# The D term by channels, and a new place for the output product, in a two-layer chunked scan on one core

## The chip, the cores and the metric

The kernel runs on one core of one Trainium2 chip. The metric is the device time of one execution in microseconds (us). A core has five engines that run side by side, each with its own instruction queue: TensorE (PE, matrix products, with a part PEld that loads weights), VectorE (DVE), ScalarE (ACT), GpSimd (POOL) and SyncE (SP, which here only issues DMA transfers). Products land in PSUM, a small accumulator memory from which DVE and ACT read.

## The reference, cut to what matters

The whole program is a network of several stages on an input of 8 x 128 x 64 x 64 numbers (8 batches, 128 channels, 4096 tokens). The change lies in one of them, the second layer's convolution part, which is built from a selective scan called `_mamba`:

```python
def _mamba(x, in_w, in_b, conv_w, conv_b, A_log, D, dt_bias, rms_w, out_w, headdim, d_state):
    zxbcdt = x @ in_w.T + in_b
    z = zxbcdt[..., :di]
    xBC = zxbcdt[..., di:2 * di + 2 * d_state]
    dt = jax.nn.softplus(zxbcdt[..., -nh:] + dt_bias)
    xp = jnp.pad(xBC, ((0, 0), (K - 1, 0), (0, 0)))
    xBC = sum((xp[:, k:k + l, :] * conv_w[:, k] for k in range(K)))     # K = 3
    xBC = _silu(xBC + conv_b)
    xs = xBC[..., :di].reshape(b, l, nh, headdim)
    Bm, Cm = xBC[..., di:di + d_state], xBC[..., di + d_state:]
    A = -jnp.exp(A_log)
    y = _ssd(xs * dt[..., None], dt * A, Bm, Cm)
    y = y + D[None, None, :, None] * xs
    y = y.reshape(b, l, di) * _silu(z)
    y = y * jax.lax.rsqrt(jnp.mean(y * y, -1, keepdims=True) + 1e-05) * rms_w
    return y @ out_w.T

def _ssd(x, A, Bm, Cm, chunk):          # per chunk
    Acs = jnp.cumsum(A, axis=-1)
    Lmat = jnp.exp(_segsum(A))          # exp(Acs[l] - Acs[s]) for s <= l
    Yd = einsum(Cm, Bm, Lmat, x)        # inside a chunk
    states = einsum(Bm, exp(Acs[-1] - Acs), x)
    st = exp(Acs[-1]) * st + states     # chunk after chunk
    Yo = einsum(Cm, previous st, exp(Acs))
    return Yd + Yo
...
gf = _mamba(gf, sm_..., 8, 16) + gf     # once, 8 channels: the "seeds"
...
def cascade(xi):                        # 8 groups of 16 channels
    for i in range(2):
        xi = _mamba(xi, cm_...[i], 8, 64)
    return xi
ys = jax.vmap(cascade)(xs) + xs * skip_scale
```

The line that the change computes in another way is `y = y + D * xs`, the D term. `xs` is the part of the projection that went through the three-tap convolution and the silu; D is one number for each head.

## The kernel before, in words

*Stages.* The program runs, one after the other: the first layer (a scan step by step), routing and experts, a set-up of the second layer (`second_setup`, which calls `ssd_weights` L989 for two layers of the cascade, CM, and for the seeds, SM), the seeds (SM), the cascade (CM), and the second feed-forward part. The tiles of the two scans end in `_cm` and `_sm` in the profile. All the parts that the change touches are used by these two.

*Tiling of the cascade.* A batch has 16 segments of SC = 256 tokens, a segment has two chunks of 128. The 8 groups of channels are held side by side: two in one 128-partition tile for B, C and states (`g2` = 2, so NP = 4 such pairs), four in one for z and y (`gh` = 4, so NH = 2 halves). A pass of the loop in `cascade` (L1575 to L1598) treats one segment of layer 0 and, two segments behind it, one of layer 1: 128 segments, 130 passes.

*A segment.* `ssd_project` (L1079) makes a segment's inputs from `stk`, the three shifted copies of the input rows stacked over partitions, so that one product does projection and convolution together: B and C (`bc_p`, into `BC`), z (`z_p` L1106 to L1111, four products, one silu into `zs`, channels on partitions), then the token products (`tok_p` L1116 to L1128: x, B and the raw dt with tokens on partitions, into `tok` and `dtr`), then after the mark `"silu"` a table load, softplus to `dt`, and `dA` = dt x A. `ssd_exponents` (L1050) sums dA along the tokens with one product (`cs_p`), splits the sum into three bf16 parts on DVE (`csq`, `csr`, L1063 to L1066: a cast, a difference, a cast, a difference) and sends them out to HBM and back in as rows `ssA`, `ssB`. Back in `ssd_project`, small products give `dec_p` (weights `wd` of the states) and `cd_p`, and `eA_p`, six products that need `csq`, gives exp of the cumulative sum with channels on partitions.

*A chunk.* `ssd_chunk` (L1173): `g_p` (products of B and C, masked by DVE into `gm`), `pad` and `xw` (x times dt, x times the state weights, on DVE), `xD` (x times D, on GpSimd, L1203 to L1205). `decays` makes the differences of the cumulative sum with rows `ssA`, `ssB` (`ss_p`, bf16 products), and ACT's exp of them into E, two tiles for each half. `masked` (L1227) multiplies E by gm on DVE. `yo_s_p` holds two things in one bank: the products of the old state with C, and the new state sums; DVE adds the latter to the scaled old state and GpSimd copies it into block form (`Sd`, L1267). After the mark `"decays"` follow y (`inside`, L1229 to L1234): for each half the product of `xD` with the identity starts the accumulation in `y_p` and the products of E and `pad` continue it. DVE multiplies yo by `eA` (`yy`), adds y, multiplies by `zs`: `yz` (L1275 to L1287).

*The output of a segment.* `ssd_output` (L1289): square on ACT, mean by products (`ms_p`), reciprocal root, the product of yz with it on GpSimd (L1302), and the output product `o_p` (L1307, two products, one for each half). `output` in `cascade` (L1516) then copies o_p out: for layer 0 on ACT into `y1s` (L1528) and by DMA to HBM, from where the next layer's `stk` is loaded (`load(1, n)`, four DMAs in `tap_stack`); for layer 1 it loads the input rows (`ys`), and DVE does x times skip plus o_p into `ys`, sums it into `gms`, and a DMA stores it.

*What sets the order.* In the cascade only ACT's table loads are pinned against the silus and exps around them (`silus_done`); for the rest the code is written as generators, each `yield` giving the turn to another, and the loop of `cascade` says which generator goes on until which mark (`until`, `between`, `both`, `drain`; `slow` gives two turns for each one). A scheduler then orders each engine's queue by the order of writing and by when inputs are ready in its own model. `after(later, earlier)` (L303) adds a dependency that fixes only the order of issue. PSUM has eight banks: tag "a" has tiles of two banks, three buffers (`wide`), for bc, z, tok, g, ss, ms and eA; tag "b" has one bank, two buffers (`narrow`), for cs, dec, cd, yo_s, y and o, which take turns in the order of writing. A new tile of a tag waits until the last reader of the tile two turns (or three) back is done. HBM rows go through SP's one queue in its order of issue.

*A pass, as it runs.* Layer 0's chunk 0, layer 1's chunk 0, layer 0's chunk 1, layer 1's chunk 1. In the first half the next segment of layer 0 is projected, in the second the next one of layer 1. Layer 0's output comes in the second half, layer 1's (`late`) is spread over the first half of the next pass.

Of the kernel before, what the change touches and what calls it, by code (L numbers as in the profile page):

```python
# [9 lines left out]
F32 = mybir.dt.float32  # L10
# [121 lines left out]
def layout(inputs):  # L132
# [74 lines left out]
    for j in range(2):  # L207
        blk = np.zeros((128, 64), np.float32)
        for g in range(4):
            blk[g * 32 : g * 32 + 32, g * 16 : g * 16 + 16] = i[p1 + "cm_out_w"][j].T  # L210
        c.add(f"cm{j}_out", blk)
        c.add(f"cm{j}_rms", np.tile(i[p1 + "cm_rms_w"][j], 4))
        c.add(f"cm{j}_Alog", rows(i[p1 + "cm_A_log"][j]))
        c.add(f"cm{j}_D", rows(i[p1 + "cm_D"][j]))
    blk = np.zeros((4, SM.nh, SM.hd, 4, SM.co), np.float32)
    rms = np.zeros((4, SM.nh, SM.hd), np.float32)
    for g in range(4):
# [2 lines left out]
    c.add("sm0_out", blk.reshape(128, 4 * SM.co))  # L220
    c.add("sm0_rms", rms.reshape(128))
    c.add("sm0_Alog", rows(i[p1 + "sm_A_log"]))
    c.add("sm0_D", rows(i[p1 + "sm_D"]))

    sd = Pack(128)
    for n in ("seed_tok_b", "seed_detok_b"):
# [52 lines left out]
class Net:  # L279
# [5 lines left out]


    def mm(self, out, lhsT, rhs, start=True, stop=True):
        self.ordered(self.nc.tensor.matmul(out, lhsT=lhsT, rhs=rhs, start=start, stop=stop))  # L288

    def keep_warm(self, bank, n):  # L290

# [697 lines left out]
    def ssd_weights(self, pool, cfg, j):  # L989

        nc = self.nc
        n = f"{cfg.name}{j}"

        def part(i):
            o, m = self.at["stacked"][f"{n}_{i}"]
            return self.st[:, o : o + m]

        W = pool.tile([128, cfg.cols], F32, name=f"W_{n}")
        nc.vector.memset(W[96:], 0.0)
        self.tt(W[:KST], part(0), part(1), ALU.mult)  # L1000
        self.tt(W[:KST], W[:KST], part(2), ALU.add)
        negA = pool.tile([128, cfg.nh], F32, name=f"negA_{n}")
        self.act(negA, self.w(f"{n}_Alog"), AF.Exp)
        self.ts(negA, negA, -1.0, ALU.mult)
        D = pool.tile([128, cfg.g2, cfg.nh, cfg.hd], F32, name=f"D_{n}")
        for g in range(cfg.g2):
            nc.vector.tensor_copy(D[:, g], bc(self.w(f"{n}_D"), cfg.hd))
        wo = pool.tile([cfg.pz, cfg.gh * cfg.co], F32, name=f"wo_{n}")
        self.ts(wo, self.w(f"{n}_out")[: cfg.pz], self.w(f"{n}_rms")[: cfg.pz], ALU.mult)
        return {"W": W, "negA": negA, "D": D.rearrange("p g h q -> p (g h q)"), "wo": wo, "fill": 6 if cfg is SM else 0}  # L1010

    def ssd_rings(self, pool, cfg, n, npads, nrows, nstates):

# [36 lines left out]
    def ssd_exponents(self, cfg, dA, n_tok, ring, wk, ps, fill):  # L1050


        nc = self.nc
        NC, nh, G = n_tok // 128, cfg.nh, cfg.g
        n = NC * G * nh
        t_ = cfg.name
        p = ps.tile([128, S], F32, tag="b", bufs=self.narrow, name="cs_p")
        self.keep_warm(p, fill)
        p = p[:n, :128]
        self.mm(p, dA.rearrange("p c g -> p (c g)"), self.k("le"))  # L1060
        part = wk.tile([n, 3, 128], BF16, name=f"csq_{t_}")
        rest = wk.tile([n, 128], F32, name=f"csr_{t_}")
        nc.vector.tensor_copy(part[:, 0], p)  # L1063
        self.tt(rest, p, part[:, 0], ALU.subtract)
        nc.vector.tensor_copy(part[:, 1], rest)
        self.tt(part[:, 2], rest, part[:, 1], ALU.subtract)  # L1066
        d = self.dp.tile([3, n, 128], BF16, name=f"cs_{t_}", bufs=3)
        nc.sync.dma_start(d.rearrange("i n t -> n i t"), part)
        A, B = self.turn(ring, "row")
        g4 = cfg.g4  # L1070
        for r in range(g4):
            v = d.rearrange("i (c g h) t -> i c g h t", g=g4, h=nh)[:, :, r]
            nc.sync.dma_start(B[32 * r : 32 * r + 3], v)
            for i in range(3):
                o = 32 * r + 3 + i * nh
                nc.sync.dma_start(A[o : o + nh, :, r], v[i].rearrange("c h t -> h c t"))
        return A, B, part

    def ssd_project(self, cfg, W, ring, stk, n_tok, wk, ps):  # L1079
# [17 lines left out]
        for j0 in range(0, NP, per):  # L1097
# [5 lines left out]
            silus.append(self.act(BC[:, j0 : j0 + per].rearrange("p j x s -> p (j x s)"),  # L1103
                                  v.rearrange("p j x s -> p (j x s)"), AF.Silu))
            yield None
        zs = wk.tile([pz, NH, n_tok], F32, name=f"zs_{t_}", bufs=nl_)  # L1106
        p = ps.tile([128, 2, S], F32, tag="a", bufs=self.wide, name="z_p")
        for j in range(NP):
            o = (j * g2 % gh) * hi
            self.mm(p[o : o + g2 * hi, j * g2 // gh, :n_tok], Wp[:, cfg.o_z : cfg.o_z + g2 * hi], stk(j))  # L1110
        silus.append(self.act(zs, p[:pz, :NH, :n_tok], AF.Silu))  # L1111
        yield None
        tok = wk.tile([128, NC, NP, cfg.wsil], F32, name=f"tok_{t_}", bufs=nb_)
        dtr = wk.tile([128, NC, NP, g2 * nh], F32, name=f"dtr_{t_}")
# [1 line left out]
        for c in range(NC):  # L1116
            p = ps.tile([128, 2, S], F32, tag="a", bufs=self.wide, name="tok_p")
            for j in range(NP):
                o = (j % ppb) * cfg.wtok
                self.mm(p[:, j // ppb, o : o + cfg.wtok], stk(j)[:, c * 128 : (c + 1) * 128],  # L1120
                        Wp[:, cfg.o_t : cfg.o_t + cfg.wtok])
            for q in range(nbk):
                v = p[:, q, : ppb * cfg.wtok].rearrange("p (j f) -> p j f", j=ppb)
                jj = slice(q * ppb, (q + 1) * ppb)
                silus.append(self.act(tok[:, c, jj, :], v[:, :, : cfg.wsil], AF.Silu))
                nc.vector.tensor_copy(dtr[:, c, jj, :], v[:, :, cfg.wsil :])  # L1126
            if c < NC - 1:
                yield None  # L1128
# [39 lines left out]
                    self.mm(p[:pz, hf, c * 128 : (c + 1) * 128], self.spread[: NC * GH, o : o + m], part[:, i],  # L1168
                            start=i == 0, stop=i == 2)
        self.act(eA, p[:pz, :NH, :n_tok], AF.Exp)  # L1170
        yield {"BC": BC, "zs": zs, "tok": tok, "dt": dt, "w": w, "cd": cd, "eA": eA, "ssA": ssA, "ssB": ssB, "n": n_tok}

    def ssd_chunk(self, cfg, W, st, sg, c, wk, ps):  # L1173

# [25 lines left out]
        xw = wk.tile([128, NP, g2 * nh, hd], F32, name=f"xw_{t_}")  # L1200
        self.tt(xw, x4, bc(w[:, c].rearrange("p (j g) -> p j g", j=NP), hd), ALU.mult)
        xw = xw.rearrange("p j g q -> p (j g q)")
        xD = wk.tile([128, NP, g2 * hi], F32, name=f"xD_{t_}")  # L1203
        self.tt(xD, xt, bc(W["D"], NP, 1), ALU.mult, nc.gpsimd)
        xD = xD.rearrange("p j q -> p (j q)")  # L1205
        yield None
        Es = [[], []]

# [18 lines left out]
                self.stt(f, f, 1.0, bc(gm[:, g0 * 128 : (g0 + ng) * 128], nh, 1), ALU.min, ALU.mult)  # L1227

        def inside(hf):  # L1229
            self.mm(y[:pz, hf], xD[:, hf * pz : (hf + 1) * pz], self.k("ident"), start=True, stop=False)  # L1230
            for h in range(nh):
                for g in range(gh):
                    self.mm(y[g * hi : (g + 1) * hi, hf], pad[:, hf * gh + g, h * hi : (h + 1) * hi],
                            Es[hf][g // ng][:, h, g % ng, :], start=False, stop=h == nh - 1)  # L1234

        old = st["S"]
        decays(0)
# [32 lines left out]
        yield "decays"  # L1270
        y = ps.tile([128, NH, 128], F32, tag="b", bufs=self.narrow, name="y_p")
        inside(0)
        if old is not None:
            yy = wk.tile([pz, NH, 128], F32, name=f"yy_{t_}")
            self.tt(yy, yo[:pz], sg["eA"][:, :, cs], ALU.mult)  # L1275
        masked(1)
        yield None
        inside(1)
# [1 line left out]
        if c == 0:  # L1280
            sg["yz"] = wk.tile([pz, NH, sg["n"]], F32, name=f"yz_{t_}")
        out = sg["yz"][:, :, cs]
        if old is None:
            self.tt(out, y[:pz], sg["zs"][:, :, cs], ALU.mult)
        else:
            self.tt(yy, yy, y[:pz], ALU.add)
            self.tt(out, yy, sg["zs"][:, :, cs], ALU.mult)  # L1287

    def ssd_output(self, cfg, W, sg, n_tok, wk, ps):  # L1289

# [13 lines left out]
        o = ps.tile([128, S], F32, tag="b", bufs=self.narrow, name="o_p")  # L1304
        n = gh * cfg.co
        for hf in range(NH):
            self.mm(o[hf * n : (hf + 1) * n, :n_tok], W["wo"], yz[:, hf])  # L1307
        yield o[: NH * n, :n_tok]

    def tap_stack(self, src, lo, first, ring):  # L1310
# [166 lines left out]
    def cascade(self, ps):  # L1477
# [5 lines left out]
        with tc.tile_pool(name="cs", bufs=1) as pl, tc.tile_pool(name="csw", bufs=2) as wk:  # L1483
# [32 lines left out]
            def output(layer, n):  # L1516
# [7 lines left out]
                if layer == 0:  # L1524
                    if k == 0:
                        y1[b] = self.dp.tile([C, L], F32, name="y1", bufs=2)
                    y = wk.tile([C, SC], F32, name="y1s")
                    nc.scalar.copy(y, o)  # L1528
                    nc.sync.dma_start(y1[b][:, sg], y)
                    load(1, n)  # L1530
                else:
                    x = wk.tile([C, SC], F32, name="ys")
                    nc.sync.dma_start(x, self.xs[b][:, sg])
                    self.stt(x, x, self.w("skip"), o, ALU.mult, ALU.add)
                    nc.vector.tensor_reduce(self.gms[:, b, k : k + 1], x, AX.X, ALU.add)
                    nc.sync.dma_start(self.ys[b][:, sg], x)
# [24 lines left out]
            def drain(*gens):  # L1561
                for g in gens:
                    for _ in g:
                        pass

            def slow(gen):

                for v in gen:
# [2 lines left out]

            load(0, 0)
            drain(project(0, 0))
            late = p = iter(())
            for n in range(total + 2):  # L1575
                x = [chunk(0, n, 0), chunk(1, n - 2, 0), chunk(0, n, 1), chunk(1, n - 2, 1)]
                until(x[0], "decays", [p])
# [3 lines left out]
                until(p, "silu")  # L1581
                drain(rest)
                until(x[1], "decays", [late])
                p = slow(p)
                next(p, None)
                until(x[1], "end", [p])
                until(x[2], "decays", [p])
                drain(p, late)
                p = project(1, n - 1)
                rest = between(x[2], x[3])  # L1590
                until(p, "silu")
                drain(rest)
                first = slow(output(0, n))
                until(x[3], "decays", [first])
                p = slow(p)
                next(p, None)
                until(x[3], "end", [p, first])
                late = both(first, slow(output(1, n - 2)))  # L1598
            drain(late)

    def second_ffn(self):

# [274 lines left out]
```

## Time and profile before

| what | value |
|---|---|
| three runs | 18963.84, 18971.56, 18972.04 us; median 18971.56 |
| the profiled execution's own time | 18991.37 us |
| its span (first to last record) | 18989.2 us |
| mean granted TensorE clock | 0.955 of full |
| busy share of PE, DVE, ACT, POOL | 85%, 81%, 59%, 48% |
| the seeds, 9487 to 10297 us | PE busy 664 of 810 us, DVE 467 |
| the cascade, 10420 to 17369 us | PE busy 6523 of 6949 us, DVE 5150, ACT 4657, POOL 1428 |

The shares over the whole span mix stages with different limits, so only the last row bears on the loop: it covers 128 passes. The busiest groups there, over 12000 to 16000 us (73 passes), each with its number of instructions, its busy time and the mean of one:

| group | engine | count | busy us | mean ns |
|---|---|---|---|---|
| E = min(E, 1) x gm, 128x1024 (L344) | DVE | 1167 | 1399.4 | 1233 |
| E = exp(ss_p), 128x1024 | ACT | 1168 | 1143.0 | 1028 |
| y_p from E and pad | PE | 18684 | 747.4 | 276 |
| ss_p | PE | 2336 | 642.5 | 381 |
| bc_p | PE | 2336 | 558.2 | 387 |
| tok_p | PE | 2336 | 434.2 | 339 |
| Sd copy, 64x128 (L1267) | POOL | 584 | 326.0 | 558 |
| xD, 128x256 | POOL | 292 | 307.3 | 1052 |
| y_p from xD and the identity | PE | 1166 | 255.2 | 301 |
| yz x sq, 128x512 (L1302) | POOL | 146 | 198.0 | 1356 |
| z_p | PE | 1168 | 158.3 | 392 |
| o_p | PE | 584 | 97.3 | 401 |
| zs = silu(z_p), 128x512 | ACT | 146 | 87.2 | 597 |

An fp32 product shows as several records, so a count here is larger than the number of products in the code. Products overlap in the pipeline, so the mean of one is more than the distance from one start to the next. Idle time of an engine is told with what ended it, "<-" and the releaser: "PE o_p <- POOL yz_cm" is time in which PE stood ahead of an o_p product until GpSimd's yz was done.

### The profile page before, as it was taken

Reading aid. Unit: us, or ns where it says so; the run is one execution under the profiler, and the core shown is the slowest. Engines: PE = TensorE matmul, PEld = TensorE weight load, DVE = VectorE, ACT = ScalarE, POOL = GpSimd, SP = SyncE. Lnnn points to the kernel's source line nnn. Section 1 sums busy time; section 2 is a strip of 40 time slices with the busy share of each in tenths; the row PEclk is TensorE's granted clock in tenths of the full one; section 3 lists DMA queues with packets and bytes.
Section 4 is the critical chain, followed back from the end, with each engine's and each line's share of the span. In section 5 each row is a group of like instructions: output and inputs, shape, how many; then the busy total and the mean of one; then the engine's idle time right before and its main releaser. Section 6 shows DMA issues by size and latency. Waiting matters only on the chain. (4 is left out here: it accounts for less than half of the span.)

```text
span 18989.2 us, 300098 instructions
## 1 busy us (share of the span) xinstructions
PE 16050.9 (85%) x114341; PEld 8381.8 (44%) x114341; DVE 15333.3 (81%) x20453; ACT 11238.5 (59%) x15902; POOL 9062.3 (48%) x6308
## 2 busy tenths in 40 slices
PE   6777777777777777777787999999999999998898
PEld 2222222222222222223644666666666666665343
DVE  6999999999999999998264777777777777776886
ACT  5555656565555656554254666666666666666553
POOL 6777777777777777774011122222222222222444
PEclk8999999999999999999697999999999999999999
DMA  3555554545555455554442011011111011011222
GB/s 108 141 142 141 141 141 137 144 139 137 143 138 138 135 145 136 137 136 119 136 145 66 27 30 30 28 30 30 28 30 29 28 30 29 28 30 37 91 94 82
DMA packets 843741, 1734.85 MB, mean 91 GB/s; under 512 B 184315, under 2 KB 416667, under 8 KB 833883
## 3 DMA queue, kind: packets, MB, share of 16 engines
q1 hardware_dynamic: 842302, 1715.66, 31.8%
q8 instruction: 904, 14.81, 0.3%
q14 instruction: 535, 4.38, 0.1%
HBM read 1474.28 MB, written 241.04 MB: 90 GB/s over the span
## 5 line engine op out<-in xcount | busy, mean ns | idle before, releaser
L335 POOL TENSOR_TENSOR bx<-xE,B 128x1024 f32<-128x1024 f32 x2048 | 4818.5, 2356 | 1032.3 <-DMA xE<-dtx_d 659.1
L288 PE MATMUL dA<-parts,expand 128*128 128x512 bf16 x12288 | 3192.5, 398 | 1846.3 <-DVE last L347 1383.8
L296 ACT ACTIVATE dA<-dA,negA 128x1024 f32<-128x1024 f32 x2048 | 2228.4, 1088 | 3224.5 <-PE dA L288 3118.6
L757 DVE TENSOR_TENSOR_SCAN dA<-dA,last,bx 128x1024 f32<-128x1024 f32 x1536 | 3609.3, 2350 | 108.5 <-POOL bx L335 90.3
L288 PEld LDWEIGHTS <-expand 128*128 128x128 bf16 x12288 | 1109.1, 100 | 4414.2 <-DVE last L347 2179.2
L296 ACT ACTIVATE E_cm<-ss_p 128x1024 f32<-128x1024 f32 x2048 | 2003.3, 1028 | 1301.1 <-PE ss_p L288 1301.0
L335 DVE TENSOR_TENSOR hc<-dA,C 128x1024 f32<-128x1024 f32 x2048 | 2507.7, 1224 | 70.4
L344 DVE SCALAR_TENSOR_TENSOR E_cm<-E_cm,gm_cm 128x1024 f32<-128x1024 f32 x2048 | 2454.7, 1233 | 86.0 <-ACT E_cm L296 45.4
L335 POOL TENSOR_TENSOR xD_cm<-tok_cm,D_cm 128x256 f32<-128x256 f32 x512 | 536.6, 1048 | 2759.8 <-PE y_p L288 2680.5
L1267 POOL COPY Sd_cm<-S_cm 64x128 f32<-64x128 f32 x1024 | 573.8, 560 | 2574.1 <-DVE S_cm L335 2467.1
L288 PE MATMUL y_p<-E_cm,pad_cm 128*32 128x128 f32 x32768 | 1316.6, 277 | 125.9 <-DVE E_cm L344 123.8
L288 PE MATMUL ss_p<-ssB_cm,ssA_cm 128*128 128x512 bf16 x4096 | 1132.1, 383 | 158.3 <-DVE gm_cm L335 96.6
L757 DVE TENSOR_TENSOR_SCAN dA<-dA,bx 128x1024 f32<-128x1024 f32 x512 | 1172.2, 2290 | 55.9 <-POOL bx L335 54.9
L288 PE MATMUL y<-hc,kt 128*32 128x512 f32 x8192 | 1207.6, 663 | 3.6 <-DVE hc L335 3.6
L1126 DVE COPY dtr_cm<-tok_p 128x16 f32<-128x16 f32 x1024 | 178.5, 174 | 1158.3 <-ACT tok_cm L296 1158.3
L288 PEld LDWEIGHTS y_p<-E_cm,pad_cm 128*32 128x32 f32 x32768 | 901.9, 109 | 429.8 <-DVE E_cm L344 247.5
L288 PE MATMUL bc_p<-stk_cm,W_cm 128*128 128x256 f32 x4096 | 985.4, 389 | 25.2 <-DMA stk_cm<-xs 20.8
L288 PEld LDWEIGHTS bc_p<-stk_cm,W_cm 128*128 128x128 f32 x4096 | 754.5, 191 | 196.4 <-issue 75.0
L288 PE MATMUL tok_p<-W_cm,stk_cm 128*128 128x200 f32 x4096 | 761.4, 339 | 0.0
L288 PE MATMUL g_p<-BC_cm 64*128 64x128 f32 x8192 | 753.1, 294 | 2.2 <-ACT E_cm L296 2.2
L296 ACT ACTIVATE tok_cm<-tok_p 128x384 f32<-128x384 f32 x1024 | 502.0, 490 | 398.2 <-PE tok_p L288 248.7
L288 PEld LDWEIGHTS tok_p<-W_cm,stk_cm 128*128 128x128 f32 x4096 | 682.5, 190 | 98.5 <-issue 98.1
(412 smaller groups left out, 29633.0 us busy)
## 6 DMA issues: line engine op xcount, KB each, us to landing
xE<-dtx_d SPq DMA_DIRECT2D x2048, 512.0 KB
dtx_d<-dtx SPq DMA_DIRECT2D x256, 256.0 KB
x<-x SPq DMA_DIRECT2D x256, 256.0 KB
pb<-p_d SPq DMA_DIRECT2D x64, 1024.0 KB
ssA_cm<-cs_cm SPq DMA_DIRECT2D x3072, 4.0 KB
stk_cm<-xs SPq DMA_DIRECT2D x368, 128.0 KB
stk_cm<-y SPq DMA_DIRECT2D x368, 128.0 KB
px<-in_x_dram SPq DMA_DIRECT2D x64, 256.0 KB
```

What stands on the lines that cost most here:

```text
L288: self.ordered(self.nc.tensor.matmul(out, lhsT=lhsT, rhs=rhs, start=start, stop=stop))
L296: i = self.ordered(self.nc.scalar.activation(out, in_, func, **kw))
L335: self.ordered((eng or self.nc.vector).tensor_tensor(out, a, b, op))
L344: self.ordered(self.nc.vector.scalar_tensor_tensor(out=out, in0=a, scalar=s, in1=b, op0=op0, op1=op1))
L757: self.ordered(nc.vector.tensor_tensor_scan(out=t, data0=t, data1=bx.pop(n), initial=0.0 if ch["j"] == 0 else last[:, q : q + 1], op0=ALU. ...
L1126: nc.vector.tensor_copy(dtr[:, c, jj, :], v[:, :, cfg.wsil :])
L1267: nc.gpsimd.tensor_copy(Sd[gr, :, g * hi : (g + 1) * hi], S2[gr])
```

## The change

The D term is computed with channels on partitions. D is packed with one number for each of the 128 partitions, and the tile D of before with its copies is dropped. `z_p` becomes twice as wide: after z's four products four more with the columns of x (`cfg.o_t`) fill its other half, and one silu over both gives `zx`, of which `zs` and `xT` (x with channels on partitions) are the halves. GpSimd multiplies xT by D once for each segment. In `ssd_chunk`, `xD` and the identity products go; the first y product of each head-0 group starts the accumulation; GpSimd adds xT to `yy` after DVE's yo x eA, and where there is no old state DVE adds xT to y itself, one operation more than before.

Two dependencies of issue order are added, both for the cascade alone: the first y product of a chunk stands behind the latest cumulative sum (`self.summed`), and the first output product behind the latest token product (`self.projected`). The loop lets layer 1's output go on for two steps only (`head`), drains the rest of it after the next token products of layer 1, and takes two steps of a projection right after the `"decays"` marks instead of one. `y1s` and `ys` share one ring of three buffers.

```diff
         c.add(f"cm{j}_Alog", rows(i[p1 + "cm_A_log"][j]))
-        c.add(f"cm{j}_D", rows(i[p1 + "cm_D"][j]))
+        c.add(f"cm{j}_D", np.tile(np.repeat(i[p1 + "cm_D"][j], CM.hd), CM.gh))
...
-        D = pool.tile([128, cfg.g2, cfg.nh, cfg.hd], F32, name=f"D_{n}")
-        for g in range(cfg.g2):
-            nc.vector.tensor_copy(D[:, g], bc(self.w(f"{n}_D"), cfg.hd))
...
-        self.mm(p, dA.rearrange("p c g -> p (c g)"), self.k("le"))
+        self.summed = self.mm(p, dA.rearrange("p c g -> p (c g)"), self.k("le"))
...
-        zs = wk.tile([pz, NH, n_tok], F32, name=f"zs_{t_}", bufs=nl_)
+        zx = wk.tile([pz, NH, 2, n_tok], F32, name=f"zx_{t_}", bufs=nl_)
         p = ps.tile([128, 2, S], F32, tag="a", bufs=self.wide, name="z_p")
-        for j in range(NP):
-            o = (j * g2 % gh) * hi
-            self.mm(p[o : o + g2 * hi, j * g2 // gh, :n_tok], Wp[:, cfg.o_z : cfg.o_z + g2 * hi], stk(j))
-        silus.append(self.act(zs, p[:pz, :NH, :n_tok], AF.Silu))
+        for x, w in enumerate((cfg.o_z, cfg.o_t)):
+            for j in range(NP):
+                o = (j * g2 % gh) * hi
+                self.mm(p[o : o + g2 * hi, j * g2 // gh, x * n_tok : (x + 1) * n_tok], Wp[:, w : w + g2 * hi], stk(j))
+        silus.append(self.act(zx.rearrange("p f x s -> p f (x s)"), p[:pz, :NH, : 2 * n_tok], AF.Silu))
+        zs, xT = zx[:, :, 0], zx[:, :, 1]
+        self.tt(xT, xT, bc(W["D"].to_broadcast([pz, n_tok]), NH, 1), ALU.mult, nc.gpsimd)
...
-                self.mm(p[:, j // ppb, o : o + cfg.wtok], stk(j)[:, c * 128 : (c + 1) * 128],
+                self.projected = self.mm(p[:, j // ppb, o : o + cfg.wtok], stk(j)[:, c * 128 : (c + 1) * 128],
                         Wp[:, cfg.o_t : cfg.o_t + cfg.wtok])
...
-        xD = wk.tile([128, NP, g2 * hi], F32, name=f"xD_{t_}")
-        self.tt(xD, xt, bc(W["D"], NP, 1), ALU.mult, nc.gpsimd)
-        xD = xD.rearrange("p j q -> p (j q)")
...
         def inside(hf):
-            self.mm(y[:pz, hf], xD[:, hf * pz : (hf + 1) * pz], self.k("ident"), start=True, stop=False)
             for h in range(nh):
                 for g in range(gh):
-                    self.mm(y[g * hi : (g + 1) * hi, hf], pad[:, hf * gh + g, h * hi : (h + 1) * hi],
-                            Es[hf][g // ng][:, h, g % ng, :], start=False, stop=h == nh - 1)
+                    i = self.mm(y[g * hi : (g + 1) * hi, hf], pad[:, hf * gh + g, h * hi : (h + 1) * hi],
+                            Es[hf][g // ng][:, h, g % ng, :], start=h == 0, stop=h == nh - 1)
+                    if cfg is CM and hf == h == g == 0:
+                        self.after(i, self.summed)
...
         inside(0)
+        yy = wk.tile([pz, NH, 128], F32, name=f"yy_{t_}")
+        xT = sg["xT"][:, :, cs]
         if old is not None:
-            yy = wk.tile([pz, NH, 128], F32, name=f"yy_{t_}")
             self.tt(yy, yo[:pz], sg["eA"][:, :, cs], ALU.mult)
+            self.tt(yy, yy, xT, ALU.add, nc.gpsimd)
...
-        if old is None:
-            self.tt(out, y[:pz], sg["zs"][:, :, cs], ALU.mult)
-        else:
-            self.tt(yy, yy, y[:pz], ALU.add)
-            self.tt(out, yy, sg["zs"][:, :, cs], ALU.mult)
+        self.tt(yy, yy if old is not None else xT, y[:pz], ALU.add)
+        self.tt(out, yy, sg["zs"][:, :, cs], ALU.mult)
...
-            self.mm(o[hf * n : (hf + 1) * n, :n_tok], W["wo"], yz[:, hf])
+            i = self.mm(o[hf * n : (hf + 1) * n, :n_tok], W["wo"], yz[:, hf])
+            if cfg is CM and hf == 0:
+                self.after(i, self.projected)
...
-                    y = wk.tile([C, SC], F32, name="y1s")
+                    y = wk.tile([C, SC], F32, name="ys", bufs=3)
...
-                    x = wk.tile([C, SC], F32, name="ys")
+                    x = wk.tile([C, SC], F32, name="ys", bufs=3)
...
+            def head(gen, k):
+                for _ in range(k):
+                    next(gen, None)
+                    yield None
+                    yield None
...
-            late = p = iter(())
+            late = out1 = p = iter(())
             for n in range(total + 2):
                 x = [chunk(0, n, 0), chunk(1, n - 2, 0), chunk(0, n, 1), chunk(1, n - 2, 1)]
                 until(x[0], "decays", [p])
...
                 until(x[1], "decays", [late])
+                next(p, None)
+                next(p, None)
                 p = slow(p)
-                next(p, None)
                 until(x[1], "end", [p])
                 until(x[2], "decays", [p])
                 drain(p, late)
                 p = project(1, n - 1)
                 rest = between(x[2], x[3])
                 until(p, "silu")
+                drain(out1)
                 drain(rest)
                 first = slow(output(0, n))
                 until(x[3], "decays", [first])
+                next(p, None)
+                next(p, None)
                 p = slow(p)
-                next(p, None)
                 until(x[3], "end", [p, first])
-                late = both(first, slow(output(1, n - 2)))
-            drain(late)
+                out1 = output(1, n - 2)
+                late = both(first, head(out1, 2))
+            drain(late, out1)
```

## The prediction

> **What bounds the kernel now.** I read the page first: span, busy slices, granted clock.
>
> ```profile
> span 18989.2 us, 300098 instructions
> ...
> PE   6777777777777777777787999999999999998898
> ...
> DVE  6999999999999999998264777777777777776886
> ...
> PEclk8999999999999999999697999999999999999999
> ```
>
> The change touches slices 20 to 36 alone: the seeds (9487 to 10297 us by the rows of E_sm) and the cascade. In the cascade PE stands at 9 in full clock. The 128 copies of L1528 start from 10419.8 to 17369.2 us: 6949.4/127 = 54.72 us per loop pass, and the passes are alike to 0.01 us away from batch edges. One pass therefore stands for the stage. Next the stretch table (us, then PE, PEld, DVE, ACT, POOL busy, clock, DMA share, GB/s):
>
> ```profile
> 12000.00:14000.00 2000.00, 1880.86 (x21824) 1353.41 (x21820) 1487.15 (x2911) 1347.88 (x1934) 413.36 (x511) 1.00 0.10 29
> ```
>
> PE is busy 94%, DVE 74%. What ends PE's idle time from 12000 to 16000 us (73 passes; total, times, longest):
>
> ```profile
> PE o_p L288 <- POOL yz_cm L335: 73.8, 73, 2.4
> PE y_p L288 <- DVE E_cm L344: 69.6, 144, 0.6
> PE ss_p L288 <- DVE gm_cm L335: 55.6, 148, 0.6
> ```
>
> That is 1.01, 0.95 and 0.76 us a pass. Two of the three are waits for DVE, so I followed one pass in order of time. PE (start, length):
>
> ```profile
> 14011.15 0.65 PE L288 MATMUL o_p<-yz_cm,wo_cm 128*64 128x256 f32 x4 [0.69 <-POOL yz_cm L335]
> ...
> 14013.22 1.08 PE L288 MATMUL z_p<-stk_cm,W_cm 128*64 128x256 f32 x8
> ...
> 14017.05 0.38 PE L288 MATMUL y_p<-kt,xD_cm 128*128 128x128 f32 x2
> 14017.36 1.08 PE L288 MATMUL y_p<-E_cm,pad_cm 128*32 128x128 f32 x32
> ...
> 14043.00 0.38 PE L288 MATMUL y_p<-kt,xD_cm 128*128 128x128 f32 x2
> ...
> 14049.87 0.43 PE L288 MATMUL cs_p<-kt,dA_cm 128*64 128x128 f32 x2
> ...
> 14051.64 0.41 PE L288 MATMUL y_p<-E_cm,pad_cm 128*32 128x128 f32 x4 [0.59 <-DVE E_cm L344]
> ```
>
> DVE and POOL:
>
> ```profile
> 14025.92 0.42 DVE L335 TENSOR_TENSOR yy_cm<-yo_s_p,eA_cm 128x256 f32<-128x256 f32 x1
> 14026.25 2.45 DVE L344 SCALAR_TENSOR_TENSOR E_cm<-E_cm,gm_cm 128x1024 f32<-128x1024 f32 x2
> ...
> 14029.24 1.34 DVE L1065 CAST csq_cm<-csr_cm 64x128 bf16<-64x128 f32 x1
> ```
> ```profile
> 14027.70 1.58 POOL L335 TENSOR_TENSOR xD_cm<-tok_cm,D_cm 128x256 f32<-128x256 f32 x1
> 14029.24 1.26 POOL L335 TENSOR_TENSOR yz_cm<-yz_cm,sq_cm 128x512 f32<-128x512 f32 x1
> ```
>
> The reader is to see two halves. Half A runs from the end of layer 1's token products (14017.05) to that of layer 0's (14043.00): 25.95 us. Half B ends at the next 14071.78: 28.78 us. After each such end ACT needs a fixed chain (silu, table load, softplus) before DVE can make dA; then DVE runs without a gap (14019.94 to 14039.6). PE fills that time, and waits for DVE where its filling runs out. So PE work taken out before such a wait turns into wait.
>
> **The change, part by part.** *Removed on PE:* eight identity products a pass. From start to next start they take 0.31 to 0.44 us (14017.05 to 14017.36, for one): 3.06 us. *Added on PE:* eight x products of z_p's shape. Four z products take 14013.22 to 14014.24 = 1.02 us, so 2.04 us. PE work falls by 1.02 us a pass. The four y_p groups lose their first accumulating write, which costs nothing.
>
> *Output product.* In the built program layer 1's o_p stands behind token products, and the wait of 1.01 us goes: yz is ready at about 14011.1, and o_p now comes 1.5 + 2.04 + 2.8 us later. But its PSUM buffer is handed on later too: the next y_p waits for DVE's ys operation, which reads it.
>
> *Order in half A* (T = 14017.05). The cumulative sum now stands ahead of y. Its PSUM buffer is that of yo_s_p, free when DVE's yy ends, 14026.34 = T+9.29; PE arrives at T+8.3 and stands, where before it did y at T+8.4. cs ends at T+9.7. Then eA_p wants csq's first cast, behind the third mask (two masks end T+11.65, so one at 10.4; 0.27 us): T+10.7. y wants ys, behind the fourth mask: 11.65 + 0.27 + 0.47 = T+12.35. PE has 1.3 us of work between T+8.3 and T+12.35: 2.7 us of new wait. From y on there remain y 2.0, dec and cd 0.6, eA 0.8, four ss pairs' rest 1.5, yo 1.0, bc 3.65, z with x 2.04, tok 2.8 and 0.4 for changes of tile shape: 14.8. Half A: 27.15 us against 25.95, +1.2.
>
> *Order in half B* (T = 14043.00). cs follows o_p directly and waits for ACT's copy out of o_p (14047.76 to 14048.81, 1.05 us in all): 0.5 us. DVE now does the four csq operations ahead of its first mask instead of behind it (14051.51 to 14052.59, 1.08 us, of which two other operations cover some 0.4). The mask ended at T+8.6; it ends at T+9.2, and y starts at T+9.25, after 1.5 us of wait. From the same y to the end PE worked 18.64 us without its waits; less xD 0.42 and o_p 0.58, plus x 1.02, less 0.4 for g products no longer split: 18.25. Half B: 27.5 against 28.78, -1.3. Together -0.1 us a pass.
>
> *POOL.* Four xD products a pass (0.73 us alone) go; four adds of the same shape and two products of 128x512 (1.26 us by yz) come: 2.5 us more, POOL going from 21% to 25%. The products run while DVE waits for tokens. The adds start when DVE's yy ends, in the middle of the masks. What that costs shows above: DVE's cast took 1.34 us while POOL's yz ran (its fellow at 14052.13 took 0.22), and POOL's xD 1.58 instead of 0.73. An add that gets in ahead of a mask (half A) or of xw (half B) pushes the chain back by up to 0.73 us; none if DVE comes first. Bounds 0 to 1.46 a pass; I take 0.6, since the trace shows both winners. Sd copies behind an add are read half a pass later: free. Should that cover go, each costs 0.78.
>
> The Trainium skill, "SBUF — State Buffer", section "SBUF: two separate sides", says GpSimd and VectorE share a port pair as an exclusive lock, taken by whichever starts first, against VectorE operations in a two-port mode or with two SBUF inputs; the rows above agree. Taken strictly it speaks against this change: every add meets masks with two SBUF inputs, and with each collision lost the pass would be 1.46 us longer instead of 0.6.
>
> *ACT.* zs of 128x512 (0.60) becomes 128x1024 (1.02 by BC): 0.43 twice a pass, ahead of the token silus, where ACT waited 1.00 us for tok_p: 0. Without that cover 0.86 a pass. *SP.* The ys load goes behind the row loads, the y1 reload behind the csq store; it is issued near T+10 of half B for a bc near T+18.8. 0; a row that came later would stop all of PE. *DVE:* same operations, bar one more in the first chunk of a batch (16 x 0.42 = 7 us at most), and six small copies of D at set-up: 0.
>
> *Seeds.* The small scan loses four identity products a segment (0.33 to 0.8 us each) and gains four of 0.28 to 0.5; the second chunk's state products move into a gap. The POOL add (0.73) and the longer silu can lie on its chain. Bounds -3 to +1 us a segment, 16 segments: I take -1, so -16.
>
> **Sum.** Cascade: (-0.1 + 0.6) x 128 = +64. Seeds -16. Edges 0. +48 on the profiled execution's 18991.4 (span 18989.2 and 2.2 around it) gives 19039. That execution lies 19.8 over the median of the runs, 18971.6, so I forecast 19,020 us.
>
> **Rivals.**
> *R1, PE alone bounds (faster).* If DVE's chain gives way, because its operations come earlier than I place them and the waits at cs, eA and y stay away, all of 1.02 + 1.01 us comes out: 2.03 x 128 = 260, and 18,695 with the seeds. For it: PE busy 94%, and o_p's wait is the largest. Against it: DVE's gapless stretch, and two of three waits. A part of it is likelier: half-way from -0.1 to -2.03, with half of POOL's 0.6, is -0.77 a pass, or 18,857.
>
> *R2, the halves cancel (not slower).* POOL's adds always come second, so that they cost nothing: -0.1 a pass, 18,943 with the seeds. With a quarter of a microsecond lost to POOL it is 18,991. For it: in the E_cm rows the mean (1233 ns) is hardly above a lone mask. Against it: the cast of 1.34.
>
> *R3, PSUM hand-over and port together (slower).* POOL's add goes ahead of the fourth mask and yz right behind it: ys ends at T+13.1 and the casts after it at T+14.3, so half A ends 0.8 us later (+2.0), and in half B xw and the state scaling lose 0.7 (-0.6): +1.4 x 128 = 180, 19,135. It decides where half A loses more than half B's 1.3. For it: cs, y and dec each wait for a buffer that DVE reads last. Against it: masks mostly win.
>
> *R4, the order isn't kept.* The built program holds both fixed places and the eight x products: chance 0.
>
> **How the numbers follow.** About 0.2% (38 us) is what a measurement of this kernel can tell from no change. The forecast proper, a loss of 0.2 to 0.7%, has 0.38; R3 and worse 0.10; R2 and all within 0.2% 0.20; R1 in part 0.24; R1 in full 0.08. So slower 0.48, same 0.20, faster 0.32. The forecast's own range, with POOL's cost from 0 to 1.46 a pass, is 18,943 to 19,130. The range over all goes from the partial R1 to R3: 18,840 to 19,140; beyond it lie full R1, the edge of the partial one and the worst, 0.2 together.
>
> **What would show it.** Right: o_p's wait for POOL gone; new PE waits cs <- DVE yy, y_p <- DVE ys and eA <- DVE csq once a pass each; y_p <- DVE E_cm above 1 us a pass; PE busy below 94%; xD gone, z_p's group doubled; a pass of 55.0 to 55.6 us. Wrong: a pass below 54.3, PE busy at 95% or more; waits on stk or ss rows; a token silu waiting for the longer one.

## The result, and the profile after

| | before | after |
|---|---|---|
| median of the runs, us | 18971.8 (4 runs) | 19229.6 (4 runs, 19197.1 to 19266.7) |
| ratio to before, 95% interval | | 1.0127, 1.0114 to 1.0141 |
| span of the profiled execution, us | 18989.2 | 19221.8 |
| start of the cascade's copies (L1528, now L1527), us | 10419.8 | 10411.7 |
| from the first of the 128 copies to the last, us | 6949.4 | 7176.9 |
| a pass in which the clock held (median), us | 54.73 (122 of 127) | 54.14 (41 of 127) |
| halved clock between these copies, by the trace's clock records, us | 48.7 | 790.1, in 108 stretches |

The change is slower by 258 us; the forecast was 19,020 us, and its range ended at 19,140. Of the 232.6 us between the spans 227.5 lie in the cascade. The page of after, span, PE and PEclk in 40 slices:

```profile
span 19221.8 us, 298995 instructions
...
PE   6778777777777777776887999999999999998898
...
PEclk8999999999999999998697999999899999998999
```

PE is busy at 9 as before, but PEclk, which was 9 in every slice of the cascade, has 8s. The stretch table shows what they are. Two passes that follow each other, from copy to copy (us, then PE, PEld, DVE, ACT, POOL busy, clock, DMA share, GB/s):

```profile
14290.72:14344.86 54.14, 48.76 (x595) 35.84 (x600) 40.91 (x81) 37.86 (x53) 16.59 (x16) 1.00 0.10 30
14344.86:14403.35 58.49, 52.94 (x595) 38.66 (x600) 41.45 (x81) 37.92 (x53) 13.99 (x16) 0.91 0.09 27
```

The same number of instructions on PE, DVE, ACT and POOL, once at full clock in 54.14 us, faster than any pass of before away from batch edges, and once at 0.91 in 58.49. Closer still: the lengths of the clock's records are multiples of 3.413 us, and a table in these steps around one fall reads (same columns):

```profile
14260.13:14263.55 3.42, 2.88 (x27) 1.93 (x24) 3.32 (x4) 3.42 (x5) 0.00 (x0) 1.00 0.01 2
14263.55:14266.96 3.41, 1.93 (x14) 1.08 (x12) 3.41 (x7) 1.30 (x3) 2.64 (x3) 1.00 0.00 0
14266.96:14270.37 3.41, 3.02 (x43) 2.37 (x44) 3.35 (x8) 0.96 (x2) 1.77 (x2) 0.50 0.13 43
14270.37:14273.79 3.42, 3.42 (x43) 2.44 (x38) 2.16 (x5) 0.20 (x1) 0.00 (x0) 0.50 0.06 15
```

In the second row PE is busy 1.93 of 3.41 us (57%), at full clock; from its end on the clock is 0.50, here for 10.24 us. The idlest stretch of that length in a pass of before:

```profile
14051.00:14054.41 3.41, 2.32 (x39) 1.74 (x42) 3.31 (x7) 2.85 (x4) 0.00 (x0) 1.00 0.66 174
```

That is 68% busy, and the clock held. PE's idle time in a pass at full clock grew from 3.1 us (54.73 us less 51.62 busy, the pass of before from 14048.44) to 5.4 (54.14 less 48.76), and the change put it together. Where it lies, in order of time on PE, half A first (just ahead of the fall above), then half B (of the pass from 14290.72, in which the clock held):

```profile
14264.51 0.43 PE L288 MATMUL cs_p<-kt,dA_cm 128*64 128x128 f32 x2 [0.68 <-DVE yy_cm L335]
...
14265.83 0.23 PE L288 MATMUL eA_p<-csq_cm,spread 64*128 64x128 bf16 x1 [0.25 <-DVE csq_cm L1060]
...
14267.35 1.06 PE L288 MATMUL y_p<-E_cm,pad_cm 128*32 128x128 f32 x13 [0.94 <-DVE ys L344]
```
```profile
14291.15 0.43 PE L288 MATMUL cs_p<-kt,dA_cm 128*64 128x128 f32 x2 [0.47 <-ACT ys L1527]
...
14293.23 0.81 PE L288 MATMUL ss_p<-ssB_cm,ssA_cm 128*128 128x512 bf16 x3 [0.47 <-ACT E_cm L296]
14295.68 0.41 PE L288 MATMUL y_p<-E_cm,pad_cm 128*32 128x128 f32 x4 [1.64 <-DVE E_cm L344]
```

Five of these waits are those of the prediction. In half A they are cs for DVE's yy, eA for csq and y for ys: 1.87 us together, where 2.7 were foretold. In half B they are cs for the copy out of o_p (0.5 foretold, 0.47) and y for the mask (1.5 foretold, 1.64). Over 12000 to 16000 us (total, times, longest):

```profile
PE y_p L288 <- DVE E_cm L344: 115.6, 71, 2.0
PE y_p L288 <- DVE ys L344: 65.0, 70, 0.9
...
PE cs_p L288 <- DVE yy_cm L335: 48.0, 70, 1.0
PE cs_p L288 <- ACT ys L1527: 30.7, 65, 0.5
```

o_p's wait for POOL yz is gone, as foretold.

### The profile page after: what moved, and what is told of

It reads as the page before. It is cut to its first block, busy times and chain, and to the rows that moved or that the text cites. A ratio compares the mean times of both kernels' runs of the same rounds, so it can differ in the third digit from the quotient of the medians.

```text
span 19221.8 us, 298995 instructions
## 1 busy us (share of the span) xinstructions
PE 15949.0 (83%) x113095; PEld 8418.5 (44%) x114277; DVE 15358.3 (80%) x20462; ACT 11374.6 (59%) x15902; POOL 9635.5 (50%) x6563
## 5 line engine op out<-in xcount | busy, mean ns | idle before, releaser
L288 PE MATMUL dA<-parts,expand 128*128 128x512 bf16 x11777 | 3150.7, 398 | 1874.9 <-DVE last L347 1385.8
L1265 POOL COPY Sd_cm<-S_cm 64x128 f32<-64x128 f32 x1024 | 729.0, 712 | 4592.4 <-DVE S_cm L335 4467.1
L288 PE MATMUL y_p<-E_cm,pad_cm 128*32 128x128 f32 x32768 | 1384.8, 300 | 322.0 <-DVE E_cm L344 206.5
L288 PEld LDWEIGHTS y_p<-E_cm,pad_cm 128*32 128x32 f32 x32768 | 1004.3, 119 | 582.4 <-DVE E_cm L344 276.1
L288 PE MATMUL ss_p<-ssB_cm,ssA_cm 128*128 128x512 bf16 x3457 | 1034.5, 390 | 208.4 <-ACT E_cm L296 92.4
L288 PE MATMUL bc_p<-stk_cm,W_cm 128*128 128x256 f32 x4096 | 942.9, 383 | 28.1 <-DMA stk_cm<-xs 20.4
L335 DVE TENSOR_TENSOR gm_cm<-g_p,kt 128x1024 f32<-128x1024 f32 x512 | 622.5, 1216 | 129.3 <-PE g_p L288 129.3
L344 DVE SCALAR_TENSOR_TENSOR dw<-h,w_second,dw 128x512 f32<-128x512 f32 x1024 | 722.8, 747 | 1.7 <-ACT h L296 1.3
```

Source lines behind the costliest of these rows:

```text
L288: return self.ordered(self.nc.tensor.matmul(out, lhsT=lhsT, rhs=rhs, start=start, stop=stop))
L335: self.ordered((eng or self.nc.vector).tensor_tensor(out, a, b, op))
L344: self.ordered(self.nc.vector.scalar_tensor_tensor(out=out, in0=a, scalar=s, in1=b, op0=op0, op1=op1))
L1265: nc.gpsimd.tensor_copy(Sd[gr, :, g * hi : (g + 1) * hi], S2[gr])
```

## The experiments

Theory C (clock): the order gains, and what is lost is the clock that falls when PE's waits come together. Theory P (port): GpSimd's added work and the hand-over of buffers make the passes longer, the clock is a sign of it and no cause. All ratios are to runs of the kernel before on the same chip; "held pass" is the median pass without halved clock, "halved" the sum in the cascade of the profiled execution.

| run | what it is | median us | ratio, 95% interval | held pass us | halved us |
|---|---|---|---|---|---|
| after | the change | 19229.6 | 1.0127 (1.0114 to 1.0141) | 54.14 | 790 |
| e1 | change, both waits filled | 18927.9 | 0.9974 (0.9962 to 0.9986) | 54.22 | 41 |
| e2 | change, half B's wait filled | 19117.8 | 1.0062 (1.0040 to 1.0083) | 54.14 | 539 |
| e3 | change, y's order undone | 19133.1 | 1.0070 (1.0053 to 1.0087) | 53.79 (7 passes) | 749 |
| e4 | D by channels alone | 19402.2 | 1.0214 (1.0199 to 1.0230) | 54.85 (3 passes) | 842 |
| e5 | before, no xD products | 18777.1 | 0.9867 (0.9841 to 0.9892) | 52.40 | 200 |
| e6 | change, no adds on GpSimd | 19328.9 | 1.0160 (1.0135 to 1.0184) | 53.68 (11 passes) | 1109 |
| e7 | order alone, D as before | 18996.6 | 0.9987 (0.9974 to 1.0001) | 54.34 | 123 |
| e8 | change, o_p's place undone | 19433.3 | 1.0218 (1.0193 to 1.0242) | 56.21 (9 passes) | 589 |
| e9 | e3, 12 dummies in half B | 18845.1 | 0.9928 (0.9912 to 0.9944) | 53.78 | 36 |
| e10 | e3, 8 dummies in half B | 18829.0 | 0.9916 (0.9903 to 0.9929) | 53.58 | 33 |
| e11 | before, the 12 dummies | 18982.3 | 0.9997 (0.9988 to 1.0005) | 54.53 | 32 |
| e12 | e6, both waits filled | 18886.5 | 0.9942 (0.9929 to 0.9955) | 53.91 | 41 |

**e1 and e2: PE is kept busy while it waits.** Dummy bf16 products go into bank space that is free at the time or overwritten by the first real product.

```diff
         self.summed = self.mm(p, dA.rearrange("p c g -> p (c g)"), self.k("le"))
+        if cfg is CM and layer == 0:
+            self.fill_y = 10
+        if cfg is CM and layer == 1:
+            for _ in range(5):            # e2: 0
+                self.mm(rest_, self.warm[:, :128], self.warm[:, 128:])
...
         def inside(hf):
+            if cfg is CM and hf == 0 and self.fill_y:
+                for _ in range(self.fill_y):
+                    i = self.mm(y.rearrange("p f l -> p (f l)"), self.warm[:, :128], self.warm[:, : NH * 128])
+                    self.after(i, self.summed)
+                self.fill_y = 0
```

> The changed kernel with dummy products on PE in its two long waits: ten of 128x256 ahead of the first y product of half B, five of 128x384 behind the cumulative sum of half A. Theory C (the clock: a stretch of 3.41 us in which PE is busy less than some 58% halves the granted clock for 3.41 to 10.24 us, and all of the loss is this): no more than 100 us of halved clock in the cascade instead of 790, a pass of 54.1 to 54.6 us instead of 56.1, and 18,890 to 18,960 us. Theory P (GpSimd's added work and the hand-over of buffers make the passes longer, and the halved clock only comes with the waits): dummies change nothing or cost their own time, 19,230 us or more.

> The changed kernel with the ten dummy products of half B alone. Theory C: half B's stretch (busy 0.38 at worst) no longer halves the clock, half A's (0.49 at worst) still does, so part of the 258 us comes back: 19,000 to 19,150 us. Theory P: 19,230 or more.

e1 is faster than before, and some 300 us faster than the change, with more work on PE and the same pass at held clock (54.22 against 54.14). Both runs came as theory C had it, and theory P falls as the cause of the loss. e2 wins back a part: 59 stretches of halved clock are left of 108, 57 of them in half A. In e1 the scheduler also moved some of half A's eA and ss products behind y; as the held pass is the same, that isn't where the gain is.

**e3, e4, e7, e8: one part at a time.** e3:

```diff
-                    if cfg is CM and hf == h == g == 0:
-                        self.after(i, self.summed)
...
-                next(p, None)
-                next(p, None)
                 p = slow(p)
+                next(p, None)
```

> The changed kernel with the order of y undone (neither the fixed place of y behind the cumulative sum nor the earlier steps of the projection); D by channels and the late output product stay. Theory C: y fills the stretch ahead of the cumulative sum again, PE's idle time is spread as before, the clock holds at 0.99 or more, and a pass takes 54 to 54.8 us: 18,880 to 18,980 us. Theory P: GpSimd has the same work as in the changed kernel, so most of the loss stays: 19,100 or more.

e4 undoes, besides, the place of o_p:

```diff
-            if cfg is CM and hf == 0:
-                self.after(i, self.projected)
...
-                drain(out1)
...
-                out1 = output(1, n - 2)
-                late = both(first, head(out1, 2))
-            drain(late, out1)
+                late = both(first, slow(output(1, n - 2)))
+            drain(late)
```

> D by channels alone: the order of the loop is that of before, nothing is fixed (the two output tiles share three buffers as in the changed kernel). Theory C: PE has 1.02 us a pass less to do and the same waits, no stretch below 58% busy: 18,940 to 18,990 us, clock 0.99 or more in the cascade. Theory P: GpSimd's adds and products cost 0.6 to 1.4 us a pass here too: 19,030 to 19,150 us.

e7 is before with all edits but those of D, and e8 is the change without those of o_p (the second diff).

> The kernel before with the new order of the loop, both fixed places and the shared ring, but with xD on GpSimd and its identity products on PE as before. Theory C: an identity product, dec and cd now stand ahead of half B's wait for the mask, so its stretch is busier than in the changed kernel (0.38); the clock is halved less often than there: 18,850 to 19,050 us. Rival O (the order by itself is the loss): 19,150 or more.

> The changed kernel with the place of layer 1's output product undone (neither fixed nor drained late); D by channels and y behind the cumulative sum stay. Theory C: half B is unchanged (busy 0.38 at worst) and the wait of o_p for yz comes back: 19,150 to 19,350 us. Rival H (the late output product holds a PSUM buffer of y for too long, and that is the loss): 18,980 to 19,080 us.

Theory C said of e3 and e4 that the clock would hold, and missed: 120 and 124 of the 127 passes have halved clock. e3's time fits theory P as well as it fits a loss to the clock; only the clock's records tell them apart. e4's lies above both. In e4, with before's order of the loop, the stretch table shows the same fall, in half B:

```profile
14120.95:14124.36 3.41, 1.28 (x5) 0.38 (x4) 3.40 (x7) 2.73 (x4) 1.49 (x3) 1.00 0.59 171
14124.36:14127.77 3.41, 3.36 (x30) 2.39 (x34) 2.06 (x3) 0.84 (x1) 0.00 (x0) 0.50 0.51 98
```

In before, three identity products of half B (0.31, 0.42 and 0.44 us from start to next start) and the cumulative sum (0.37) stood ahead of the wait for the mask, 0.59 us in the prediction's rows. The third of them:

```profile
14049.43 0.38 PE L288 MATMUL y_p<-kt,xD_cm 128*128 128x128 f32 x2
```

In e4 the identity products are gone, and the cumulative sum stands behind the wait:

```profile
14124.41 0.64 PE L288 MATMUL y_p<-E_cm,pad_cm 128*32 128x128 f32 x4 [1.88 <-DVE E_cm L344]
14124.98 0.69 PE L288 MATMUL cs_p<-kt,dA_cm 128*64 128x128 f32 x2
```

So PE has 1.5 us less filling there, waits 1.88 us, and 38% busy is left. D by channels brings the fall by itself; the order isn't needed for it. e7, with the identity products, has 123 us of halved clock and is no slower than before, as theory C had it.

What each part does at held clock is known only roughly, for the held passes of e3 (all seven) and e4 (two of three) are the second ones of a batch, where before's pass is 54.40 us and not 54.73. Compared at that place, D by channels costs 0.45 us a pass (54.85), and the late output product takes off 1.06 (53.79). What y behind the cumulative sum costs stays open: no pass of the change held at that place (e2 has 55.02 there, with its dummies), and none of e3 anywhere else. e8 missed as well (19,433 us; theory C's range ended at 19,350), but shows o_p's place again: with y behind the cumulative sum and o_p early, the wait of o_p for yz comes back with 2.2 us a pass (154.5 us in 69), and the held pass is 56.21.

**e5: work left out of before.** The two lines of `inside` with xD go, `start=h == 0`.

> The kernel before with its identity products of xD left out of PE (so the D term is missing from y in the cascade and the seeds); nothing else is edited, GpSimd still makes xD. PE has 3.06 us a pass less to do. Theory C: the products stood as filling ahead of PE's waits for the mask; without them a stretch of 3.41 us falls below 58% busy, the clock is halved once a pass in many passes, and the kernel gets slower although work is left out: 19,050 to 19,400 us. Theory W (waits alone, no clock): the work removed turns into wait or into gain, 18,600 to 18,980 us, never slower.

A miss for theory C: 236 us faster than before on the same chip. The eight products (3.06 us a pass) are worth 2.33 us at held clock, so PE's work did bound before's pass far more than the prediction had it; and only 36 of the 127 passes have halved clock, although the idlest 3.41 us of a pass are 48% busy. Theory C's "58%" of any 3.41 us is no fixed border.

**e6 and e12: the adds on GpSimd.** The one line `self.tt(yy, yy, xT, ALU.add, nc.gpsimd)` goes, from the change and from e1.

> The changed kernel without GpSimd's four adds a pass (the D term is missing wherever there is an old state); the projection, its silu and the product with D stay. Theory C: PE's two stretches stay below 58%, so the halved clock stays, and only the port's cost goes (up to 0.5 us a pass, by the state scaling of 0.73 us against 0.28): 19,130 to 19,230 us. Theory P: the adds are the loss, 18,880 to 18,990 us.

> The changed kernel with both waits filled and without GpSimd's adds (the D term is missing wherever there is an old state). Theory C with a cost for the port: at full clock the pass without the adds took 53.65 us against 54.14 with them, so with the clock held it gains 0.4 to 0.5 us a pass over the filled kernel with adds (18,928): 18,840 to 18,890 us. Rival N (the adds cost nothing): 18,900 to 18,960 us.

e6 lies above both ranges. Its cascade takes 78 us longer than the change's in the profiled executions (7255.1 us from the first copy to the last), although its held pass is shorter by 0.46 us: 84 of its passes carry the full 10.24 us of halved clock. With the clock held (e12 against e1) leaving out the adds gains 0.31 us a pass and 41 us, as theory C had it. What they do to DVE shows in the state scaling, first row e1, second e12 (count, busy us, mean ns):

```profile
L336 DVE TENSOR_TENSOR S_cm<-S_cm,cd_cm 128x128 f32<-128x128 f32 x285 | 184.3, 647 | 0.0
```
```profile
L336 DVE TENSOR_TENSOR S_cm<-S_cm,cd_cm 128x128 f32<-128x128 f32 x287 | 79.9, 278 | 0.0
```

The masks did not wait for the adds: one took 1234 ns in e1 and 1237 in e12. It is the add that took long, 1437 ns on average in e1, where an xD of the same shape took 730 alone.

**e9, e10 and the control e11.** Twelve or eight dummies, fixed behind the last ss product:

```diff
+            if cfg is CM and hf == 0 and c == 0 and st["layer"] == 1:
+                for _ in range(8):
+                    i = self.mm(y.rearrange("p f l -> p (f l)"), self.warm[:, :128], self.warm[:, : NH * 128])
+                    self.after(i, self.lagged)   # the last ss product
```

> The kernel with y's order undone (D by channels, late output product) and twelve dummy products of 128x256 on PE behind the last ss product of half B, in PE's wait for the first mask (1.9 us there). Theory C: at full clock its passes took 53.79 us; with that one stretch filled the clock holds (under 80 us halved in the cascade instead of 749), a pass takes 53.8 to 54.0 us, and the whole 18,840 to 18,900 us, the best of all that compute everything. Rival P or O: the dummies add 1.3 us of work a pass, 19,130 or more.

> The same with eight dummies (about 0.9 us). Theory C: the stretch goes from 38% busy to about 64%, at the border, so the clock holds in most passes: 18,840 to 18,980 us. Rival: 19,100 or more.

> Control: the kernel before with the same twelve dummies at the same place, where its clock holds already. Theory C: nothing to gain; PE waits 0.6 us there, so up to 0.7 us a pass is added: 18,980 to 19,080 us. If dummies or the order that comes with them sped things up by themselves: below 18,930 us.

e10 in order of time on PE:

```profile
14020.77 1.28 PE L288 MATMUL ss_p<-ssB_cm,ssA_cm 128*128 128x512 bf16 x5 [0.42 <-DVE gm_cm L335]
14021.89 1.04 PE L288 MATMUL y_p<-warm 128*128 128x256 bf16 x8
14023.95 0.41 PE L288 MATMUL y_p<-E_cm,pad_cm 128*32 128x128 f32 x4 [1.02 <-DVE E_cm L344]
```

A microsecond of useless work fills the first half of the wait, 1.02 us of it are left, and the clock holds. The kernel is 0.84% faster than before, and some 300 us faster than e3. e9 and e11 lie in theory C's ranges; e10 is a little faster than its own. Twelve do no better than eight. In before, where the clock holds anyway, the same twelve change nothing (0.9997).

## Why the prediction was wrong

**The step that failed** is the first reading: "In the cascade PE stands at 9 in full clock." I took that clock over into the changed kernel, priced each new wait at its own length, and no rival had it otherwise. The waits came where they were foretold, but three of them lie within some 3.5 us in half A, and in half B 1.64 us stand in one piece; there the clock is halved. 127 intervals of the held pass, 54.14 us, would be 6876 us; measured were 7176.9: 301 us for the clock, 0.38 us for each microsecond of halved clock. e1, in which the clock held, confirms it by a run: 6880.1 us. The order and D gave 127 x 0.59 = 75 us at held clock. The sum, +226, is near the 227.5 of the table (it leaves aside batch edges and the 48.7 us of halved clock in before). e1, e10 and e11 show that it is the clock and not the waits.

**The sign** came right by luck. Slower had 0.48, for a loss of half a microsecond a pass; at held clock the change is faster by 0.59, and the loss came from a term that the sum had at nothing. The held pass lies below 54.3 us, which the prediction named as a sign that it is wrong, and the average one, 56.5, above its 55.0 to 55.6.

**The halves** were near: 27.01 us for A (27.15 foretold) and 27.13 for B (27.5), from the last token products at 14285.88, 14313.01 and 14340.02 us. But these contain what GpSimd costs, for which I added another 0.6. Without adds the pass takes 53.68 us, against 54.65 by my halves: PE's work and waits were taken 1.0 us a pass too high. The rows show where. With T at the product that follows the tokens, as in the prediction, y starts at T+12.57 in half A and T+9.54 in half B, 0.5 us later together than foretold; what follows it takes 14.44 and 17.59 us instead of 14.8 and 18.25, 1.0 us less together.

**GpSimd** was mis-sized: 0.46 us a pass unfilled and 0.31 filled, against 0.6, and it wasn't the masks that paid. The rule of the Trainium skill's "SBUF — State Buffer", section "SBUF: two separate sides", holds for the single instruction: four state scalings a pass take 0.37 us more each beside the adds (647 against 278 ns), 1.48 us of DVE time. That this is near the 1.46 of the strict reading is chance, for that one stood for two whole collisions with a mask or with xw. The pass gets only 0.31 to 0.46 of it.

**The output product**: 1.01 us priced as gone; e4 to e3 measures 1.06. **D on PE**: 1.02 us less work, of which nothing came: by e4, D by channels costs 0.45 us at held clock. The added products, silu and adds can have taken it back; no run parts them. **Seeds**: -16 foretold, and not seen: from their first mask to their last they took 810.0 us before, 823.1 after, and 829.2 in e11, whose seeds are those of before, so the difference says nothing. The cascade started 8.1 us earlier because the stages ahead of the seeds, which the change hardly touches, were done 24 us earlier. **Rivals**: R1's full gain isn't there (-0.59 of -2.03 us a pass, even at held clock); R2 and R3 argued about tenths of a microsecond in a pass that lost 2.4 on average to the clock; R2's 18,991 for a quarter of a microsecond lost should be 18,975, as it leaves out the seeds; R4's chance of 0 was right.

## What to carry to other kernels

When an edit takes filling work from TensorE ahead of a wait, or sets waits side by side, look at PE's busy share in steps of 3.41 us along one pass, and not over the stage: here 94% over 2000 us held the clock, with no step under 68% away from batch edges, and 90% (1808.7 of 2000 us) with steps at 38% did not. If a wait can't be filled with real work, about 1 us of dummy bf16 products in it cost nothing that shows here (e11) and was worth 300 us. And compare variants at held clock as well as by their time, or the fall of the clock is taken for the cost of the edit.

## What the runs showed of the hardware

The throttle acts on waits well short of what one would look for. The Trainium skill, "TensorE: Matmul & The Clock Gate", section "Why this matters for your kernels", warns of idle gaps over some 3 us; here, away from batch edges, the longest single wait in the 3.41 us ahead of a fall was 1.0 us in half A and 2.0 in half B. The measurement decides: waits of 0.25 to 0.94 us that come close together are enough. The page's free-running window of 3413 ns (its section "What's actually happening") agrees with the records: the lengths are multiples of it, and in every run all falls of the cascade lie on one grid of 3413.3 ns, to within 1 or 2 ns.

So it matters how an idle stretch lies on that grid. In the change the passes that held have the same idlest 3.41 us as those with a fall, 38% busy (medians of 33 and 55 passes away from batch edges). Half B of the held pass from 14290.72, first its idlest step, then the two steps of the grid that share it (columns as before):

```profile
14292.27:14295.68 3.41, 1.30 (x7) 0.29 (x4) 3.38 (x10) 2.73 (x3) 1.48 (x3) 1.00 0.17 49
14290.85:14294.27 3.42, 2.37 (x9) 0.89 (x10) 3.38 (x10) 1.68 (x3) 1.70 (x3) 1.00 0.25 77
14294.27:14297.68 3.41, 2.00 (x34) 1.62 (x38) 3.41 (x4) 2.56 (x4) 0.00 (x0) 1.00 0.28 82
```

The grid cuts the 38% into 69% and 59%, and the clock holds.

A pass's length then decides how often its idle stretch falls into one window whole, and a fall makes the pass longer, so the loop locks on to the grid. A held pass of 54.14 and a slow one of 58.49 us make 112.63 us, 33 windows, and the pair repeats: 102.4 us full, 10.24 us halved. Six passes of the change in a row took about 61.44 us, 18 windows, with two falls in each. In e6 75 of the 127 passes took 58.03 us, 17 windows, with a fall in each, which is how shorter passes got more halved clock. A pass of e5 takes 52.40 us, 15.35 windows, so its stretch at 48% lies whole in a window only now and then. A pass made longer or shorter on purpose wasn't tried.

What exactly the throttle counts stays open. Taking the windows that end where the clock's records change, the busy share that best parts falls from none is 0.58 in the change, but 0.46 in e3, 0.49 in e4 and e5, 0.66 in e6 and 0.71 in e7; so the busy share of the profile is only near to its measure.
